# Products over the latent values in two wider bursts, with paired query products

## The chip, the cores and the metric

The kernel runs on one core of one Trainium2 chip. The metric is the device time of one execution in microseconds (us): 1379.67 before the change, the median of three runs (1377.71 to 1380.4). A core has a matrix engine (TensorE, PE in the profile), a vector engine (VectorE, DVE), a scalar engine (ScalarE, ACT), a general engine (GpSimd, POOL) and a queue that issues transfers (SyncE, SP). Each takes its own instructions strictly in their order and waits on semaphores for the others.

## The reference

Two transformer layers over 1024 tokens of width 256, in float32. Each is an attention and a block of experts, both behind a modulated layer norm and added back with a gate. What the change touches is the first attention of the first layer, which works on low-rank latents:

```
q_mid = rmsnorm(h @ q_a_w.T)                     # 192 wide
q = (q_mid @ q_b_w.T) per head: q_nope (128), q_pe (64)
kv = rmsnorm(h @ kv_a_w[:64].T)                  # 64 latents a token
k_pe = h @ kv_a_w[64:].T per head (64)
k_nope, v = kv @ kv_b_w.T per head (128, 128)
q_pe, k_pe = apply_rope(q_pe), apply_rope(k_pe)
probs = softmax((q_nope.k_nope + q_pe.k_pe) * scale)     # 16 heads
main = concat(probs @ v) @ o_w.T
```

Beside it stands a small second attention ("pattern") whose output is mixed in with a gate for each token.

## The kernel before

**Absorbed weights.** The up-projections are folded into the queries and into the output. A head's query is 128 numbers for each token: 64 that meet the 64 latents, and 64 rotated ones that meet the rotated keys. A score is one product over 128 rows. The values are the 64 latents themselves, and what the probabilities make of them is multiplied by a folded output weight, wvo. q_mid lies in q0T (its first 128 rows) and in rows 0 to 63 of mixT; rows 64 to 127 of mixT hold the latents.

**Units.** The stage runs over 16 units: 8 pairs of heads, and for each pair two halves of 512 queries (i = 0, 1). A unit has eight steps: four tiles of 128 queries for each of the two heads. A step n does these things:

- `scores(n + 2)`: two products of 128 x 128 by 512 keys into a score tile (`score_products`, line L686), the negated maximum on DVE (L690), and the exponential on ACT, which also sums (L869).
- `transposed(n)`: DVE transposes blocks of 32 x 32 of the probabilities (L877), so that keys come to stand on partitions, four groups of 32.
- Work kept in a table by step (`at(...)`): for the unit before, `over_latents` in four parts at steps 1 to 4 of the next unit; `by_latent` (four transposes on PE at L891 and ACT's copy bc at L895), which brings the inverse sums (L883, L885) into the layout of the products; and `out_part`, the four output products (L926) with an accumulation on DVE (L927).
- For the next pair of heads: `query_part` twice a unit, once for the rotated part and once for the latent part, and, where i = 0, `key_part` for both halves of the keys. `turned` rotates: ACT scales the product into t (L629) and copies four strips of 32 partitions into sw (L633), each into its partner's place; POOL multiplies and adds (L636, L637, L640). The latent part is copied straight by ACT (L675, L676).

**The products over the latents.** The array is used as eight small ones: four row groups of 32 keys and two column groups of 64. In `over_latents` row group r takes its 32 keys of block b, loads the 64 latents of those keys as weights, and streams 128 columns (four query tiles of 32 queries) of one head; column group j is head j. The four row groups add up in four PSUM tiles, and at the end DVE multiplies each of these by its piece of bc into cx (L919). One part is 8 blocks x 4 row groups x 2 heads = 64 products, in the profile 128 records, since each float32 product is two records.

**Buffers.** PSUM has two score tiles (sc) of two banks, and four tiles of one bank under the names nn and mm, handed out in turn. A unit's four row-group tiles take all four of these from the first part to the last.

**What sets the order.** In this stage only PE's order is written out by hand, by the step table. The orders of ACT, DVE and POOL are laid by a planner at build time; on the chip each engine then keeps to that order.

Of the kernel before, what the change touches and what calls it, by code (L numbers as in the profile page):

```python
# [8 lines left out]
F32 = mybir.dt.float32  # L9
# [5 lines left out]
P = 128  # L15
T = 1024
# [26 lines left out]
def adaln_two_layers(ctx: ExitStack, tc: tile.TileContext, a: dict, out: bass.AP):  # L43
    nc = tc.nc
# [7 lines left out]
    sc_tile = lambda: psum.tile([P, T], F32, tag="sc", name="sc")  # L52
    singles = ["nn", "mm"]

    def mm_tile(tag=None):
        if tag is None:
            tag = singles[0]
            singles.reverse()
        return psum.tile([P, 512], F32, tag=tag, name=tag)

    turn = [0]
# [433 lines left out]
    with pool("l0a") as l0, pool("mla") as ml:  # L495
        lnw = l0.tile([P, 2], F32, name="lnw")
        gate_b = l0.tile([P, 2], F32, name="gate_b")
        q0T = l0.tile([P, T], F32, name="q0T")
        mixT = l0.tile([P, T], F32, name="mixT")
# [5 lines left out]
        scale = (DN + DR) ** -0.5  # L505

        wq0 = l0.tile([P, NH, KVR], F32, name="wq0")
        wq1 = l0.tile([P, NH, KVR], F32, name="wq1")
# [3 lines left out]
        kv32 = ml.tile([P, 4 * NT, KVR], F32, name="kv32")  # L512
# [102 lines left out]

        kf = [[x[j].rearrange("p t d -> p (t d)") for j in range(2)], None]
        mp, wts, scs = [None], {}, {}
        qfs = {(0, 0): [l0.tile([P, 512], F32, tag=f"qf{j}", name="qf") for j in range(2)]}

        def turned(dst, at, ps, i, mul, early):  # L620
# [29 lines left out]
        def key_part(p, i, early=False):  # L650
            cols = slice(i * 512, (i + 1) * 512)
            ps = mm_tile()
            for k in range(2):
                nc.tensor.matmul(ps, wts[p][0][:, k, :], hT[i][:, k, :], start=(k == 0), stop=(k == 1))
            yield from turned(kf[p % 2], cols, ps, i, 1.0, early)

        def query_part(p, i, turn, early=False):


            cols = slice(i * 512, (i + 1) * 512)  # L660
            ps = mm_tile()
            if turn:
                if (p, i) != (0, 0):
                    qfs[p, i] = [mp[0].tile([P, 512], F32, tag=f"qf{j}", name="qf", bufs=3) for j in range(2)]
                w0, w1 = wts[p][1][:, 0, :], wts[p][1][:, 1, :]
            else:
                w0 = wq0[:, 2 * p : 2 * p + 2, :].rearrange("p h m -> p (h m)")
                w1 = wq1[:, 2 * p : 2 * p + 2, :].rearrange("p h m -> p (h m)")
            nc.tensor.matmul(ps, w0, q0T[:, cols], start=True, stop=False)
            nc.tensor.matmul(ps, w1, mixT[:, cols], start=False, stop=True)  # L670
            if turn:
                yield from turned(qfs[p, i], slice(0, 512), ps, i, scale, early)
            else:
                copy = nc.vector.tensor_copy if early else nc.scalar.copy
                copy(qfs[p, i][1][0:64, :], ps[0:64, :])  # L675
                copy(qfs[p, i][0][64:128, :], ps[64:128, :])  # L676
                yield

        def score_products(n):

# [13 lines left out]
        with pool("pat") as pat:  # L694
# [11 lines left out]
            with pool("absorb") as ab:  # L706
# [8 lines left out]
                with pool("first") as fp:  # L715
# [26 lines left out]
                    qT, kT, v = small_tensors(pat)  # L742
                    late = []
                    firsts, step, n_steps, last_divided = small_attention(pat, qT, kT, v, False, late)
                    nc.gpsimd.memset(wq1[64:128], 0.0)


                    nc.scalar.activation(own4[0:1, 0:1], one, AF.Silu)
# [1 line left out]
                    ps = mm_tile()  # L750
# [97 lines left out]
        with pool("mla1") as m1, pool("mla2", 2) as m2:  # L848
# [3 lines left out]
            def latents_of_odd():  # L852
                nc.gpsimd.tensor_copy(kf[1][0][64:128, :], mixT[64:128, :])
                nc.scalar.copy(kf[1][1][0:64, :], mixT[64:128, :])

            prs, sums, pts, cxs, bcs, rws, avs = {}, {}, {}, {}, {}, {}, {}


            units = [(p, i) for p in range(NH // 2) for i in range(2)]
# [12 lines left out]
            def transposed(n):  # L872

                u, t, j = n // 8, n % 8 // 2, n % 2
                if n % 8 == 0:
                    pts[u] = [m2.tile([P, T // 32, P], F32, tag=f"pt{k}", name="pt") for k in range(2)]
                nc.vector.transpose(  # L877
                    pts[u][j][:, :, 32 * t : 32 * t + 32], prs.pop(n).rearrange("p (b k) -> p b k", k=32)
                )

            def one_over_sums(u):
# [15 lines left out]
            def over_latents(u, part):  # L897


                n = T // 32 // 4  # L900
                if part == 0:
                    avs[u] = [mm_tile() for _ in range(4)]
                pt, av = pts[u], avs[u]
                for b in range(n * part, n * part + n):
                    for r in range(4):
                        row = slice(32 * r, 32 * r + 32)
                        for j in range(2):
                            nc.tensor.matmul(  # L908
                                av[r][64 * j : 64 * j + 64, :P], kv32[row, b, :], pt[j][row, b, :],
                                start=(b == 0), stop=(b == 4 * n - 1),  # L910
                            )
                if part < 3:
                    return
                del pts[u], avs[u]
                cxs[u] = m2.tile([P, 4, P], F32, name="cx")
                bc = bcs.pop(u)
                for r in range(4):
                    q = slice(32 * r, 32 * r + 32)
                    nc.vector.tensor_mul(  # L919
                        cxs[u][:, :, q], av[r][:, :P].rearrange("p (t q) -> p t q", t=4), bc[:, :, q]  # L920
                    )

            def out_part(u, t):
                p, i = units[u]
# [10 lines left out]
            def at(n, fn, *args):  # L935
                beside.setdefault(n, []).append((fn, args))


            def over_tiles(n, parts):

                for k in range(3):
                    at(n + k, lambda: next(parts, None))

            for u, (p, i) in enumerate(units):
                n = 8 * u
                if u + 1 < len(units):
                    at(n + 8, by_latent, u)
                for part in range(4):
                    at(n + 9 + part, over_latents, u, part)
                    if u + 1 == len(units) and part == 1:  # L950

                        at(n + 9 + part, by_latent, u, lambda: sc_tile()[:, :512])
                for t, m in enumerate((14, 15, 16, 16)):
                    at(n + m, out_part, u, t)
                if p + 1 < NH // 2:
                    if i == 0:
                        at(n, weights_of, p + 1)
                    over_tiles(n + 5, query_part(p + 1, i, True))
                    over_tiles(n + 6, query_part(p + 1, i, False))
                    if i == 0:  # L960
                        over_tiles(n + 6, key_part(p + 1, 0))
                        over_tiles(n + 7, key_part(p + 1, 1))
            def reload():
                for i in range(2):
                    nc.sync.dma_start(x[i], xv[:, 4 * i : 4 * i + 4, :])

            over_tiles(1, query_part(0, 1, True))
            over_tiles(3, query_part(0, 1, False))
            at(4, latents_of_odd)
            at(112, reload)  # L970
            last = 8 * len(units)
            at(last, residual, 0, gates_bc[0][:, :HID])
# [320 lines left out]
    with tc.manual_schedule(engines={mybir.EngineType.PE}):  # L1293
        wts = [golden(0), None]
# [16 lines left out]
        parts = projections(0, [0], False)  # L1311
# [177 lines left out]
```

## Time and profile before

| what | before |
|---|---|
| median of three runs | 1379.67 us |
| profiled execution | 1377.59 us |
| its span, first to last instruction | 1375.8 us |
| granted TensorE clock | 0.992 |
| first score to last product over latents | 316.8 to 818 us |
| 13 units between 371.2 and 774.5 us | 403.3 us |
| two successive units in the steady state | 62.03 us |

In the lines from the profile, L908 is line 908 of the kernel above. A group's line gives the engine, what it writes and reads, shapes, how many there were, busy time and mean duration in ns, then the engine's idle time before these instructions and what ended it. In a timeline the first column is the start in us from the span's start and the second the length of the merged run of instructions; a wait stands in brackets with its releaser. Matrix products overlap in their pipeline, so what one costs PE is the distance to the next start, not the listed duration.

### The profile page before, as it was taken

To read this page: it belongs to the slowest core of one execution; us is meant where nothing else is said; L and a number is where in the kernel's file an instruction comes from. 1 tells how busy PE (TensorE), PEld (TensorE's weight loads), DVE (VectorE), ACT (ScalarE), POOL (GpSimd) and SP (SyncE) were. 2 spreads that over 40 slices of the span, in tenths; PEclk is the share of its full clock that TensorE was granted. 3 is DMA by queue.
4 is the path that set the end of the run, shared out by engine and by line. 5 is a ranking of instruction groups with operands and counts; after the bars stand their busy time and mean duration, and the time that the engine had idled before them with its cause. 6 is when DMAs were issued, how large, how long until landed. Compare 5 with 4: busy or idle time off the path is not lost. (4 is left out here: it accounts for less than half of the span.)

```text
span 1375.8 us, 33066 instructions
## 1 busy us (share of the span) xinstructions
PE 1316.5 (96%) x14664; PEld 723.0 (53%) x14664; DVE 821.1 (60%) x1259; ACT 603.7 (44%) x1083; POOL 206.6 (15%) x194
## 2 busy tenths in 40 slices
PE   8999999998999999999999989999999998999998
PEld 6543324324555555555555565565556454466665
DVE  3668887836676676767676764444466666143222
ACT  4436665655655646454655323111034644511111
POOL 2000000041424324141424011000000031010000
PEclk9999999999999999999999999999999999999999
DMA  9210000000000000000001202222120000224441
GB/s 261 76 33 1 1 1 1 1 1 16 10 2 10 6 7 6 6 6 6 2 3 41 71 16 70 81 75 77 59 59 22 2 1 1 92 91 149 151 155 54
DMA packets 56601, 59.34 MB, mean 43 GB/s; under 512 B 15047, under 2 KB 42184, under 8 KB 56458
## 3 DMA queue, kind: packets, MB, share of 16 engines
q1 hardware_dynamic: 55914, 57.22, 13.7%
q8 instruction: 115, 1.88, 0.5%
q14 instruction: 28, 0.23, 0.1%
q10 hardware_dynamic: 544, 0.00, 0.0%
HBM read 55.05 MB, written 1.12 MB: 41 GB/s over the span
## 5 line engine op out<-in xcount | busy, mean ns | idle before, releaser
L323 DVE TENSOR_REDUCE mx<-sc 128x2 f32<-128x1024 f32 (+3 forms) x224 | 239.9, 1106 | 52.0 <-PE sc L317 18.1
L869 ACT ACTIVATE pr<-sc,nmax 128x1024 f32<-128x1024 f32 x128 | 142.5, 1113 | 216.3 <-DVE nmax L690 210.1
L877 DVE STREAM_TRANSPOSE pt<-pr 128x1024 f32<-128x1024 f32 x128 | 158.9, 1242 | 122.1 <-ACT pr L869 122.1
L317 PE MATMUL sc<-kT,qT 32*128 32x512 f32 (+3 forms) x896 | 208.4, 594 | 21.0 <-DVE mx L323 20.8
L351 PE MATMUL mm<-q,kT 32*128 32x512 f32 (+3 forms) x388 | 193.1, 603 | 3.3 <-DVE t L627 1.7
L351 PE MATMUL nn<-q,kT 32*128 32x512 f32 (+3 forms) x388 | 192.5, 606 | 0.7 <-DVE qf L676 0.5
L690 DVE TENSOR_REDUCE nmax<-sc 128x1 f32<-128x1024 f32 x128 | 153.8, 1203 | 14.2 <-PE sc L686 10.8
L908 PE MATMUL mm<-pt,kv 32*64 32x128 f32 x4096 | 135.2, 274 | 5.2 <-ACT bc L895 5.2
L361 ACT ACTIVATE pt<-mm 128x512 f32<-128x512 f32 (+2 forms) x194 | 108.3, 558 | 71.4 <-PE nn L351 47.8
L908 PE MATMUL nn<-pt,kv 32*64 32x128 f32 x4096 | 135.4, 274 | 4.3 <-issue 3.0
L908 PEld LDWEIGHTS mm<-pt,kv 32*64 32x64 f32 x4096 | 117.2, 130 | 30.1 <-issue 23.1
L908 PEld LDWEIGHTS nn<-pt,kv 32*64 32x64 f32 x4096 | 116.9, 130 | 28.2 <-issue 21.8
L361 ACT ACTIVATE pt<-nn 128x512 f32<-128x512 f32 (+2 forms) x194 | 108.3, 558 | 53.1 <-PE mm L351 21.0
L686 PE MATMUL sc<-kf,qf 128*128 128x512 f32 x256 | 124.0, 607 | 1.1 <-ACT pr L869 1.1
L686 PE MATMUL sc<-x,qf 128*128 128x512 f32 x256 | 123.3, 606 | 1.4 <-ACT pr L869 1.4
L317 PEld LDWEIGHTS sc<-kT,qT 32*128 32x128 f32 x896 | 68.2, 186 | 103.4 <-DVE mx L323 87.3
L636 POOL TENSOR_TENSOR t<-t,cos 128x512 f32<-128x512 f32 x32 | 41.2, 1289 | 523.5 <-ACT sw L633 267.8
L1243 DVE TENSOR_TENSOR he<-he,row 128x512 f32<-128x512 f32 x46 | 31.7, 692 | 132.9 <-ACT he L1235 99.9
L1235 ACT ACTIVATE he<-sc,b 128x512 f32<-128x512 f32 x43 | 29.5, 687 | 123.7 <-PE sc L1234 123.7
L1234 PE MATMUL sc<-hT,w 128*128 128x512 f32 x172 | 80.7, 593 | 0.0
L633 ACT COPY sw<-t 32x512 f32<-32x512 f32 x116 | 71.4, 616 | 2.0
L686 PEld LDWEIGHTS sc<-x,qf 128*128 128x128 f32 x256 | 45.5, 189 | 50.5 <-issue 46.4
(361 smaller groups left out, 2014.9 us busy)
## 6 DMA issues: line engine op xcount, KB each, us to landing
w<-in_moe_w_dram SPq DMA_DIRECT2D x50, 256.0 KB
w<-in_wg_dram SPq DMA_DIRECT2D x16, 256.0 KB
w<-in_wu_dram SPq DMA_DIRECT2D x16, 256.0 KB
w<-in_wd_dram SPq DMA_DIRECT2D x16, 256.0 KB
row<-gD SPq DMA_DIRECT2D x14, 256.0 KB
wm<-in_wmod_dram SPq DMA_DIRECT2D x6, 512.0 KB
x<-in_x_dram SPq DMA_DIRECT2D x4, 512.0 KB
wo<-in_o_dram SPq DMA_DIRECT2D x1, 2048.0 KB
```

The lines of the kernel that those rows point to most:

```text
L317: nc.tensor.matmul(sc[:, i, :n], qT[r, g, qt * P : (qt + 1) * P], kT[r, g, c * 512 : c * 512 + n], start=True, stop=not diag,)
L323: nc.vector.tensor_reduce(mx[:, qi, c, 2 * pair : 2 * pair + 2], sc[:, :, :n], AX.X, ALU.max)
L351: nc.tensor.matmul(ps[:, q0:], kT[r, g, kc * P : (kc + 1) * P], state[u]["q2"][r, q0:], start=True, stop=not diag,)
L361: nc.scalar.activation(pt[:, 2 * pair + i, q0:], ps[:, q0:], AF.Exp)
L633: copy(sw[32 * (s ^ 1) : 32 * (s ^ 1) + 32, :], t1[32 * s : 32 * s + 32, :])
L636: nc.gpsimd.tensor_mul(t1, t1, cos[:, cols])
L686: nc.tensor.matmul(sc[:, c], qfs[p, i][j][:, t * P : (t + 1) * P], kf[p % 2][j][:, c], start=True, stop=True)
L690: nc.vector.tensor_reduce(nmax, sc, AX.X, ALU.max, negate=True)
L869: nc.scalar.activation(pr, sc, AF.Exp, bias=nmax, accum_out=sums[u][:, t, j : j + 1])
L877: nc.vector.transpose(pts[u][j][:, :, 32 * t : 32 * t + 32], prs.pop(n).rearrange("p (b k) -> p b k", k=32))
L908: nc.tensor.matmul(av[r][64 * j : 64 * j + 64, :P], kv32[row, b, :], pt[j][row, b, :], start=(b == 0), stop=(b == 4 * n - 1),)
L1234: nc.tensor.matmul(ps, w1[:, k, :], hT[i][:, k, :], start=(k == 0), stop=(k == 1))
```

## The change

The products over the latents:

- The two column groups no longer stand for the two heads. Column group c takes every other block of 32 keys, and each product streams both heads' columns, 256 instead of 128. A unit has half as many products, each twice as wide, in two parts (steps 1 and 3) instead of four.
- Head j's sum is therefore split over both column groups. The transposed probabilities lie in one tile with four slots, so placed that column group 0 streams head 0 then head 1, and column group 1 head 1 then head 0. At the end ACT copies the first 128 columns of each row group's tile, two DVE adds bring in the crossed halves, and one multiplication of the whole by bc runs on POOL (for the last unit on DVE).

The queries:

- `query_parts` makes both query products of a unit at one step and in two tiles: the two with 128 rows first, then the two last chunks of 64 rows, one on rows 64 to 127 (latent part) and one on rows 0 to 63 (rotated part). For this, rows 0 to 63 of wq1 and of mixT are copied into their rows 64 to 127 once (`last_of_q_mid_twice`); a clearing of wq1's lower rows on POOL goes.
- Query pieces before that copy run their last chunk on rows 0 to 63 alone.

The table: the later pieces of the keys' rotation are put at steps further on, and `by_latent` of the last unit goes ahead of its second part.

```diff
+        def query_products(ps, p, i, turn, k):
+            lower = both[0] and not turn and k
+            row = (slice(0, P), slice(64, P) if lower else slice(0, 64))[k]
+            if turn:
+                w = wts[p][1][row, k, :]
+            else:
+                w = (wq0, wq1)[k][row, 2 * p : 2 * p + 2, :].rearrange("p h m -> p (h m)")
+            q = (q0T, mixT)[k][row, i * 512 : (i + 1) * 512]
+            nc.tensor.matmul(ps, w, q, start=(k == 0), stop=(k == 1))
...
+        def query_parts(p, i):
+            qfs[p, i] = [mp[0].tile([P, 512], F32, tag=f"qf{j}", name="qf", bufs=3) for j in range(2)]
+            pts = [mm_tile() for _ in range(2)]
+            for k in range(2):
+                for turn in range(2):
+                    query_products(pts[turn], p, i, turn, k)
+            parts = turned(qfs[p, i], slice(0, 512), pts[1], i, scale, False)
+            next(parts)
+            latent_dims(p, i, pts[0])
+            yield
+            yield from parts
...
-                    nc.gpsimd.memset(wq1[64:128], 0.0)
...
+            def last_of_q_mid_twice():
+                both[0] = True
+                nc.vector.tensor_copy(wq1[64:128], wq1[0:64])
+                nc.vector.tensor_copy(mixT[64:128, :], mixT[0:64, :])
...
-                    pts[u] = [m2.tile([P, T // 32, P], F32, tag=f"pt{k}", name="pt") for k in range(2)]
+                    pts[u] = m2.tile([P, T // 64, 4, P], F32, name="pt")
+
                 nc.vector.transpose(
-                    pts[u][j][:, :, 32 * t : 32 * t + 32], prs.pop(n).rearrange("p (b k) -> p b k", k=32)
+                    pts[u][:, :, slice(1, 3) if j else slice(0, 4, 3), 32 * t : 32 * t + 32],
+                    prs.pop(n).rearrange("p (b c k) -> p b c k", c=2, k=32),
                 )
...
-                n = T // 32 // 4
+                n = T // 32 // 2
...
-                for b in range(n * part, n * part + n):
+                for b in range(n * part, n * part + n, 2):
                     for r in range(4):
                         row = slice(32 * r, 32 * r + 32)
-                        for j in range(2):
+                        for c in range(2):
                             nc.tensor.matmul(
-                                av[r][64 * j : 64 * j + 64, :P], kv32[row, b, :], pt[j][row, b, :],
-                                start=(b == 0), stop=(b == 4 * n - 1),
+                                av[r][64 * c : 64 * c + 64, : 2 * P], kv32[row, b + c, :],
+                                pt[row, b // 2, 2 * c : 2 * c + 2, :].rearrange("p j q -> p (j q)"),
+                                start=(b == 0), stop=(b + 2 == 2 * n),
                             )
...
-                    nc.vector.tensor_mul(
-                        cxs[u][:, :, q], av[r][:, :P].rearrange("p (t q) -> p t q", t=4), bc[:, :, q]
-                    )
+                    by = [av[r][:, k * P : (k + 1) * P].rearrange("p (t q) -> p t q", t=4) for k in range(2)]
+                    nc.scalar.copy(cxs[u][:, :, q], by[0])
+                    for j in range(2):
+                        row, other = (slice(64 * k, 64 * k + 64) for k in (j, 1 - j))
+                        nc.vector.tensor_add(cxs[u][row, :, q], cxs[u][row, :, q], by[1][other])
+                eng = nc.vector if u + 1 == len(units) else nc.gpsimd
+                eng.tensor_mul(cxs[u], cxs[u], bcs.pop(u))
...
-                for part in range(4):
-                    at(n + 9 + part, over_latents, u, part)
+                for part in range(2):
...
+                    at(n + 9 + 2 * part, over_latents, u, part)
...
-                    over_tiles(n + 5, query_part(p + 1, i, True))
-                    over_tiles(n + 6, query_part(p + 1, i, False))
+                    over_tiles((n + 5, n + 6, n + 7), query_parts(p + 1, i))
                     if i == 0:
-                        over_tiles(n + 6, key_part(p + 1, 0))
-                        over_tiles(n + 7, key_part(p + 1, 1))
+                        over_tiles((n + 6, n + 8, n + 9), key_part(p + 1, 0))
+                        over_tiles((n + 7, n + 10, n + 11), key_part(p + 1, 1))
...
+            at(4, last_of_q_mid_twice)
```

## The prediction

> **What bounds the kernel now.** I read the page first (who is busy, costliest groups), then the busy time by stretch, then the timeline of TensorE (PE) and of ScalarE (ACT) over one unit.
>
> ```profile
> PE 1316.5 (96%) x14664; PEld 723.0 (53%) x14664; DVE 821.1 (60%) x1259; ACT 603.7 (44%) x1083; POOL 206.6 (15%) x194
> ...
> L908 PE MATMUL mm<-pt,kv 32*64 32x128 f32 x4096 | 135.2, 274 | 5.2 <-ACT bc L895 5.2
> ```
> ```profile
> 371.20:774.50 403.30, 394.41 (x7384) 224.70 (x7381) 285.03 (x338) 219.79 (x373) 126.30 (x100) 1.00 0.05 15
> ```
>
> The second fence is busy time from 371.2 us (end of unit 0's last burst) to 774.5 (unit 13's): length, then PE, weight loads, DVE, ACT, POOL. PE works through 394.4 of 403.3 us and the granted clock is 1.00: PE sets the pace of these thirteen units. What one item costs it is the distance between starts, not the duration of a row:
>
> ```profile
> 599.76 1.88 PE L686 MATMUL sc<-x,qf 128*128 128x512 f32 x4
> 601.48 0.59 PE L926 MATMUL mm<-wvo,cx 128*128 128x256 f32 x2
> 601.91 0.59 PE L926 MATMUL nn<-wvo,cx 128*128 128x256 f32 x2
> 602.35 0.60 PE L891 MATMUL mm<-ident,rw 128*128 128x128 f32 x4
> 602.78 1.88 PE L686 MATMUL sc<-x,qf 128*128 128x512 f32 x4
> 604.59 0.32 PE L908 MATMUL nn<-pt,kv 32*64 32x128 f32 x2
> ...
> 605.93 0.33 PE L908 MATMUL mm<-pt,kv 32*64 32x128 f32 x2 [0.88 <-ACT bc L895]
> ...
> 607.84 1.98 PE L686 MATMUL sc<-x,qf 128*128 128x512 f32 x4
> 609.75 0.32 PE L908 MATMUL nn<-pt,kv 32*64 32x128 f32 x2
> ...
> 611.78 1.98 PE L686 MATMUL sc<-x,qf 128*128 128x512 f32 x4
> ```
>
> A score is 601.48 - 599.76 = 1.72 us, an output product 0.43, the four transposes 0.43. With a burst behind it a score takes 609.75 - 607.84 = 1.91, and a burst 611.78 - 609.75 = 2.03. A burst is 64 products over 8 array tiles, each two records of 128 columns: 16 rounds of 0.109 (the spacing of the 128-column L891) = 1.74. So each visit to the small tiles costs 0.28 + 0.19 = 0.47 beyond its arithmetic. The burst at 604.59 takes 3.25: it waits until 605.93 for ACT's copy bc. ACT's timeline says why:
>
> ```profile
> 596.80 0.60 ACT L629 ACTIVATE t<-nn 128x512 f32<-128x512 f32 x1
> 597.43 2.50 ACT L633 COPY sw<-t 32x512 f32<-32x512 f32 x4
> 599.95 1.12 ACT L869 ACTIVATE pr<-sc,nmax 128x1024 f32<-128x1024 f32 x1
> 600.96 0.19 ACT L869 ACTIVATION_READ_ACCUMULATOR pr<-sc,nmax 128x1 f32 x1
> 601.05 0.59 ACT L629 ACTIVATE t<-nn 128x512 f32<-128x512 f32 x1
> 601.67 2.50 ACT L633 COPY sw<-t 32x512 f32<-32x512 f32 x4
> 604.20 1.11 ACT L869 ACTIVATE pr<-sc,nmax 128x1024 f32<-128x1024 f32 x1
> 605.21 0.19 ACT L869 ACTIVATION_READ_ACCUMULATOR pr<-sc,nmax 128x1 f32 x1
> 605.30 0.58 ACT L895 COPY bc<-mm 128x512 f32<-128x512 f32 x1
> ```
>
> For some 10 us ACT works without a gap: a scaled copy and four exchange copies (3.14 in all), an exponential (1.11), and again, with bc last. Units with i = 0 make keys too ("key units", 33.27 us from burst end to burst end, this stall in them); the others ("plain", 28.76) have no such wait. 7 x 28.76 + 6 x 33.27 = 400.9; the rest of the 403.3 is a 1.86 us hole in the burst at 763.7, no engine named, and 0.4 in the first.
>
> **The change part by part.** *Two bursts instead of four.* The same columns stream: 16 rounds x 0.216 (the record spacing of the 256-column L926) = 3.46 per burst, + 0.28 = 3.74, + 0.19 on the score before. Two cost 7.86 where four cost 8.88: -1.0 per unit. The Trainium skill (TensorEngine Tiling, Instruction Overhead) states about 60 cycles beyond the columns for each matmul; by that estimate 256 records fewer, spread over 8 tiles, would give 0.8 more per unit (13 us in all). The rows contradict it: 128 columns 0.109, 256 columns 0.216. I take nothing for the smaller count.
>
> *Queries.* Four products of 0.86 (3.44) become two of 0.86 and a pair on 64 rows each, side by side. No row shows a 64-row pair; the nearest are the 32-row L317 and L351, whose four products start within 0.02 us of each other and repeat after 0.53. So 0.86 for the pair and two switches of 0.2: 2.98, -0.46. Bounds: 3.84 if the pair runs one after the other, 2.58 with free switches.
>
> *Evacuation.* Four DVE multiplies (0.2 apart) become four ACT copies (128 columns, about 0.25 each, between the 0.27 of L361's shortest and its spacing), eight DVE adds at 0.2 and one POOL multiply (1.28, L636). From the burst's end that is 2.2 on DVE, then POOL until 3.6. The skill's rule that speaks against the change (TensorEngine Tiling, PSUM Bottleneck) is that tiling leaves evacuation as the limit. Queued behind the new waits are, on ACT, the exponential of the first score (wanted at 3.5, copies done at 1.3), on DVE that score's maximum (1.9, delayed to 2.2) and on POOL the query multiplies (10.7). The first query product needs the first buffer at 3.4 and the first output product needs cx at 8.1: both are covered, by two scores and by the query block. Without that cover, taken as the limit, with PE waiting out the 2.2, it would be +1.4 per unit. I take 0.
>
> *Transposes* keep 32-element runs, with another stride between them: 1.24 kept. DVE per unit, from start to next start: eight maxima at 1.11 and transposes at 1.17, adds 1.6, four accumulations (L927) at 0.38, the sums' inverse and its spread 0.65: 22.0 of about 30.
>
> *Exchanges.* They are spread in the program, but the built order of ACT keeps all four copies directly behind their scaled copy, and in both kinds of unit both latent copies (0.58 + 0.60) now stand ahead of them: query work is one lump of 0.58 + 0.60 + 3.14 = 4.32 ahead of the next exponential. Time zero is a unit's last burst end. A score's maximum starts 0.2 after it, its exponential 1.32 after that (620.30 to 625.94 in DVE's timeline holds such a row of steps), and each score takes one of two buffers, free again when the exponential ends.
>
> Plain unit. PE: two scores 3.44, queries to 6.42, score C to 8.14, output, score D, output: 10.72. ACT: lump 6.43 to 10.75; behind it in the queue stands C's exponential, which could have begun at 9.7, and runs to 11.87. The fifth score needs C's buffer: it starts at 11.95, a stall of 1.23 (late next is D's exponential, 12.98, and nothing waits for it). Then 1.72 + 0.86 + 0.44 + 1.91 + 3.74 + 1.72 + 1.91 + 3.74 = 16.04: 28.0 instead of 28.76.
>
> Key unit. After the queries at 6.42 PE has three scores (5.16), two key products (3.44), four output products (1.72), the transposes (0.44) and the score before the burst (1.91): 19.09. ACT: 10.75 + 1.11 + 3.14 + 1.11 + 3.14 + 1.11 + bc 0.58 = 20.94. The burst loses 1.8, since three of its four row groups have buffers and do 0.1 of it before. Late next are DVE's transposes of those scores; they end at 32.2, just ahead of the next evacuation. Then 3.74 + 1.72 + 1.91 + 3.74: 32.0 instead of 33.27.
>
> Sum: 7 x 28.0 + 6 x 32.0 = 388.0, + 0.9 (half of the 1.86 hole; half as many instructions to fetch may be its cure, but nothing shows it) = 388.9 against 403.3: -14.4. Unit 14 has no queries and hangs on the score buffers: its third score waits for the first's exponential (4.7) and its fifth for the third's (9.9), with 16.0 behind that: 25.9 instead of 26.57, -0.65. Start (316.8 to 371.2): two visits fewer, one pair, -1.4; the two earlier query pieces run their last chunk on 64 rows alone, two switches of 0.2 each, of which half on the path, +0.4; the copy of 64 x 1024 into mixT (0.69, L790) lies on DVE where PE waits little: 0 to +0.7, taken as 0. The same copy of wq sits in DVE's queue at 65.7 ahead of two maxima: +0.4, of 0 to 0.7; the POOL memset removed (0.95, at 4.9) is waited for by nobody. Tail: two visits fewer -1.0, but copies, adds and a DVE multiply follow one another before the last output products, +1.0: 0, of -1 to +2. Behind it the engines' order is unchanged. Total: -1.4 + 0.4 + 0.4 - 14.4 - 0.65 = -15.7, say -16. The profiled execution is 1377.59 (span 1375.8 and 1.8 around it), 2.1 below the median; the difference goes on the median: 1379.67 - 16 = 1363.5.
>
> **Rivals.** A, the exchanges don't stall PE: 26.77 and 30.2 per unit, another 7 x 1.23 + 6 x 1.8 = 19.4: 1344. For it: PE is the only engine above 75% in the stretch. Against it: ACT's order, and a bc wait of 0.88 already there with the same work. B, the 64-row pair runs in sequence: +0.86 in 14 units, 12 us: 1375.5. For it: the form isn't in the trace; against it the 32-row rows. C, slower: the strided write makes the transpose dearer. Each 0.1 us is 0.8 per unit; DVE's 22.0 fills the 30 at +1.0, and from about +1.1 (2.3 instead of 1.24) a unit passes the 31.0 of before. At double cost DVE has 31.4, with some waits left about 33: 14 x 2 = +28, 1408. Against it: same run length, same count of elements.
>
> **How the numbers follow.** Forecast 0.67, A 0.12, B 0.13, C 0.08. The forecast's own range is 1356 to 1370 (0.5 us per unit either way); A's 1338 to 1350, B's 1371 to 1380. The range 1347 to 1377 leaves out C and the outer parts of A and B. A difference under 0.2% (2.8 us) can't be told from none: faster 0.89, same 0.03, slower 0.08.
>
> **What would show it.** Distances: score to score 1.91 and a burst 3.74; query block 2.98; a stall of about 1.2 ended by an exponential (pr) before a plain unit's fifth score; bc ending a wait of nearly 2 us in each key unit's first burst; transposes at 1.24. The prediction is wrong if ACT's lump doesn't reach PE, if the pair's products start 0.4 apart, or if DVE shows no gaps.

## The result and the profile after

The changed kernel takes 1364.82 us in the median (four runs, 1364.39 to 1368.62), against 1379.62 for the kernel before beside it: ratio 0.9901, with a 95% interval of 0.9881 to 0.9921. Taken again later it was 0.9890 (0.9873 to 0.9906). The change makes the kernel 1.0% faster; the forecast was 1363.5, with 1347 to 1377 as its range.

The profiled execution took 1364.39 us, span 1362.6. The first lines of the page after (busy time of each engine; costliest groups of the products over the latents):

```profile
PE 1297.5 (95%) x10568; PEld 694.6 (51%) x10568; DVE 848.4 (62%) x1326; ACT 616.7 (45%) x1147; POOL 224.3 (16%) x208
...
L936 PE MATMUL mm<-pt,kv 32*64 32x256 f32 x2048 | 124.5, 381 | 5.6 <-ACT bc L923 5.5
```

The busy time by stretch, for the thirteen units between the last bursts of units 0 and 13, for unit 14, and from there to the first product of the experts (start and end, length, then PE, weight loads, DVE, ACT, POOL, with the granted clock as the third number from the end):

```profile
370.35:757.96 387.61, 374.06 (x4061) 199.73 (x4053) 304.82 (x391) 229.94 (x424) 142.33 (x113) 1.00 0.05 14
757.96:784.06 26.10, 24.07 (x309) 13.31 (x301) 23.09 (x31) 10.83 (x21) 1.26 (x1) 1.00 0.01 2
784.06:812.12 28.06, 22.90 (x316) 15.59 (x309) 21.17 (x49) 5.92 (x15) 3.94 (x8) 0.88 0.04 9
```

Thirteen units take 387.6 us where they took 403.3, and PE's share of them is 374.1 of 387.6, where it was 394.4 of 403.3: PE has less to do, and waits a little more. Of these three lines only the last has a clock below 1.00. Start distances of PE in the steady state give 27.96 us for a plain unit (forecast 28.0, before 28.76) and 31.98 for a key unit (forecast 32.0, before 33.27).

PE in a plain unit of the changed kernel:

```profile
373.89 1.02 PE L668 MATMUL nn<-q0T,wq 128*128 128x512 f32 x2
374.75 1.02 PE L668 MATMUL mm<-q0T,wpe 128*128 128x512 f32 x2
375.70 0.69 PE L668 MATMUL nn<-mixT,wq 64*128 64x512 f32 x1
375.70 0.69 PE L668 MATMUL mm<-mixT,wpe 64*128 64x512 f32 x1
...
376.76 1.98 PE L708 MATMUL sc<-kf,qf 128*128 128x512 f32 x4
378.58 0.59 PE L958 MATMUL nn<-wvo,cx 128*128 128x256 f32 x2
379.01 1.88 PE L708 MATMUL sc<-kf,qf 128*128 128x512 f32 x4
...
382.47 0.70 PE L708 MATMUL sc<-kf,qf 128*128 128x512 f32 x1 [1.15 <-ACT pr L895]
```

The two 64-row products start together (375.70), and the query block takes 376.76 - 373.89 = 2.87, with 0.10 more on the score behind it: 2.97, forecast 2.98. The fifth score then waits 1.15 for an exponential; from start to start the output product ahead of it takes 382.47 - 380.73 = 1.74 instead of 0.43, so the stall costs 1.31 (forecast 1.23). ACT in the same unit shows the lump, the six copies of the query work that stand together:

```profile
376.86 0.58 ACT L672 COPY qf<-nn 64x512 f32<-64x512 f32 x1
377.45 0.58 ACT L673 COPY qf<-nn 64x512 f32<-64x512 f32 x1
378.06 0.60 ACT L630 ACTIVATE t<-mm 128x512 f32<-128x512 f32 x1
378.68 2.50 ACT L634 COPY sw<-t 32x512 f32<-32x512 f32 x4
381.21 1.12 ACT L895 ACTIVATE pr<-sc,nmax 128x1024 f32<-128x1024 f32 x1
```

The exponential that the score waits for runs from 381.21 to 382.32, that is 10.86 to 11.97 after the last burst's end at 370.35; the forecast had 10.75 to 11.87. In a key unit the same work makes bc late in the first burst:

```profile
417.86 0.65 PE L936 MATMUL nn<-pt,kv 32*64 32x256 f32 x4
419.42 0.43 PE L936 MATMUL mm<-pt,kv 32*64 32x256 f32 x2 [0.91 <-ACT bc L923]
```

That burst takes 5.64 instead of 3.64, so the wait costs 2.0 (forecast 1.8); the 0.91 is only what is left after three of the four row groups have done what they could.

### The profile page after: what moved, and what is told of

Read it like the earlier page. It is cut to its first block, busy times and chain, and to the rows that moved or that the text cites. A ratio compares the mean times of both kernels' runs of the same rounds, so it can differ in the third digit from the quotient of the medians.

```text
span 1362.6 us, 25036 instructions
## 1 busy us (share of the span) xinstructions
PE 1297.5 (95%) x10568; PEld 694.6 (51%) x10568; DVE 848.4 (62%) x1326; ACT 616.7 (45%) x1147; POOL 224.3 (16%) x208
## 4 chain that ended last, share of the span: by engine, by line
PE 73%; ACT 12%; DVE 10%; issue 2%; SPq 1%; DMA 1%; POOL 0%; DVEq 0%; ACTq 0%
PE sc L317 10%; PE sc L708 8%; PE mm L936 6%; PE sc L1267 5%; PE mm L383 5%; ACT pr L895 5%; DVE mx L323 4%; ACT sw L634 4%; PE sc L1151 4%; PE nn L1283 3%; PE nn L936 3%; PE mm L1283 3%; PE nn L383 2%; DVE cx L951 2%; PE mm L1151 2%
## 5 line engine op out<-in xcount | busy, mean ns | idle before, releaser
L904 DVE STREAM_TRANSPOSE pt<-pr 128x1024 f32<-128x1024 f32 x128 | 157.0, 1236 | 51.5 <-ACT pr L895 51.5
L936 PE MATMUL mm<-pt,kv 32*64 32x256 f32 x2048 | 124.5, 381 | 5.6 <-ACT bc L923 5.5
L708 PE MATMUL sc<-kf,qf 128*128 128x512 f32 x256 | 120.7, 604 | 6.6 <-ACT pr L895 6.6
L936 PE MATMUL nn<-pt,kv 32*64 32x256 f32 x2048 | 124.9, 382 | 1.9 <-DVE pt L904 1.9
L936 PEld LDWEIGHTS mm<-pt,kv 32*64 32x64 f32 x2048 | 85.2, 133 | 29.3 <-issue 11.7
L936 PEld LDWEIGHTS nn<-pt,kv 32*64 32x64 f32 x2048 | 84.9, 133 | 20.1 <-issue 12.3
L708 PEld LDWEIGHTS sc<-kf,qf 128*128 128x128 f32 x256 | 45.6, 189 | 62.3 <-issue 55.2
```

Source lines behind the costliest of these rows:

```text
L708: nc.tensor.matmul(sc[:, c], qfs[p, i][j][:, t * P : (t + 1) * P], kf[p % 2][j][:, c], start=True, stop=True)
L904: nc.vector.transpose(pts[u][:, :, slice(1, 3) if j else slice(0, 4, 3), 32 * t : 32 * t + 32], prs.pop(n).rearrange("p (b c k) -> p b c k ...
L936: nc.tensor.matmul(av[r][64 * c : 64 * c + 64, : 2 * P], kv32[row, b + c, :], pt[row, b // 2, 2 * c : 2 * c + 2, :].rearrange("p j q -> p ...
```

## The experiments

The table gives, for each kernel whose units differ, the steady distances from a unit's last burst to the next one's, and the time; the runs that only change the stage's end follow in their section. The sections below say what each was.

| kernel | plain unit | key unit | both | median us | ratio to before (95%) |
|---|---|---|---|---|---|
| before | 28.76 | 33.27 | 62.03 | 1379.62 | |
| changed | 27.96 | 31.98 | 59.94 | 1364.82 | 0.9901 (0.9881 to 0.9921) |
| wide bursts alone | 27.42 | 31.87 | 59.29 | 1358.91 | 0.9853 (0.9830 to 0.9876) |
| query part alone | 29.57 | 33.49 | 63.06 | 1387.71 | 1.0063 (1.0048 to 1.0078) |
| changed, ACT's order by hand | 28.86 | 30.02 | 58.88 | 1364.39 | 0.9896 (0.9881 to 0.9910) |
| the same, key steps moved | 27.76 | 30.02 | 57.78 | 1352.50 | 0.9804 (0.9785 to 0.9823) |
| the same, ten products at the end | 27.76 | 30.02 | 57.78 | 1350.49 | 0.9786 (0.9768 to 0.9804) |
| the same, 64-row products not paired | 28.59 | 31.26 | 59.85 | 1364.88 | 0.9890 (0.9871 to 0.9909) |
| query part alone, ACT's order by hand, key steps moved | 28.88 | 31.59 | 60.47 | 1372.17 | 0.9944 (0.9931 to 0.9957) |
| wide bursts, four visits a unit | 30.25 | 34.8, 38.06 | | 1416.43 | 1.0256 (1.0226 to 1.0286) |

### Which part of the change pays

The wide bursts alone: the changed kernel with the queries, the keys' steps and the clearing of wq1 put back.

```diff
-                    over_tiles((n + 5, n + 6, n + 7), query_parts(p + 1, i))
+                    over_tiles(n + 5, query_part(p + 1, i, True))
+                    over_tiles(n + 6, query_part(p + 1, i, False))
...
-            at(4, last_of_q_mid_twice)
```

> The change without its query part: wide products in two bursts and the new evacuation, but the queries, the keys' rotation and the clearing of wq1 as before the change. By the prediction's sum the bursts are worth -1.0 per unit and the hole -1.9, so about -17 over the stage, less the 5 that the tail gave back in the changed kernel: 1379.6 - 12 = 1367 to 1368. Plain unit 27.8 (28.76 before), key unit 32.3 (33.27 before), bursts 3.64 with 1.91 on the score before them. If instead the wide products themselves are worth nothing and the gain came from the queries: 1379, plus the tail's 5, 1384. If the evacuation through ACT, DVE and POOL costs PE something that the query part only covered: above 1372.

Measured: 1358.91, units of 27.42 and 31.87, some 9 us below what I expected and 5.9 us *faster than the whole change*. The two units gain 2.74, 1.37 for each, where I had 1.0. What PE waited for in the units, first in the changed kernel and then in this one (what waits and for whom, us in total, times, longest):

```profile
PE sc L708 <- ACT pr L895: 8.1, 7, 1.2
PE mm L936 <- ACT bc L923: 5.5, 6, 0.9
```

```profile
PE mm L910 <- ACT bc L897: 2.6, 6, 0.4
```

Without the query part no score waits for an exponential, and bc is late by 0.4 instead of 0.9. The evacuation through ACT, DVE and POOL is in both.

The query part alone, on the kernel before:

```diff
-                    over_tiles(n + 5, query_part(p + 1, i, True))
-                    over_tiles(n + 6, query_part(p + 1, i, False))
+                    over_tiles((n + 5, n + 6, n + 7), query_parts(p + 1, i))
...
+            at(4, last_of_q_mid_twice)
```

> The query part of the change alone: paired 64-row products, the copies into rows 64 to 127 and the new steps of the keys' rotation, on the kernel before with its four bursts. If the pair's gain of 0.5 per unit reaches the end: 14 x 0.5 = 7, 1372 to 1373. If ACT's lump (both latent copies and four exchange copies ahead of the next exponential) stalls PE here as in the changed kernel, 1.1 in a plain unit's fifth score and more at a key unit's bc, the gain is eaten: 1378 to 1386, with a wait ended by pr in the fifth score of a plain unit. I hold the second for likelier.

Measured: 1387.71, slower than before by 0.63% (0.48 to 0.78). Its waits:

```profile
PE sc L708 <- ACT pr L895: 8.1, 7, 1.2
PE mm L934 <- ACT bc L921: 6.7, 6, 1.1
PE mm L934 <- issue: 2.2, 1, 2.2
```

The same wait of 1.15 in each plain unit as in the changed kernel (8.1 in 7). The pair saves 0.46 and the lump that comes with it costs 1.31 from start to start: a plain unit gets longer by 0.81. (The line with "issue" is a wait inside a burst for which the profile names no releaser, like the hole of 1.86 before the change.) So the change is one part that gains about 1.4 per unit and one that gives 0.1 to 0.5 of it back (0.2 to 0.8 on the kernel before).

### Is it ACT's order?

The changed kernel with ACT's order in this stage laid by hand, as the program has it. Nothing else moves.

```diff
-            with tc.manual_schedule(engines={mybir.EngineType.PE}):
+            with tc.manual_schedule(engines={mybir.EngineType.PE, mybir.EngineType.Activation}):
```

> The changed kernel with ACT's order in this stage written out as the program has it, so that the exchange copies really stand two and two behind later exponentials. If the lump of six copies is what stalls PE (the forecast's mechanism; its absence was rival A): the waits of 1.15 in the fifth score and of 0.9 to 2 at bc go, plain unit 26.8 to 27.0, key unit 30.2 to 30.6, and 19 in all: 1345 to 1348. If PE's stalls have another cause, or another copy takes the lump's place: 1360 to 1366.

Measured: 1364.39, as good as no change, and yet the two waits that I had named are gone. Key units fall to 30.02, what rival A gave them (30.2). Plain units rise to 28.86, and the waits say for whom:

```profile
PE sc L708 <- POOL kf L641: 5.0, 4, 1.3
PE sc L708 <- POOL x L641: 3.8, 3, 1.3
```

In program order the last two exchange copies of the second key half stand at step 11, behind the four copies of cx. In one such unit they are done at 494.6, but on POOL the multiplies for that half now stand behind the one for cx, which waits for DVE until 496.1: they start at 497.3, and the score that needs these keys waits 1.26. At the stage's start PE waits 1.92 once for the copy into mixT, which now waits for the latents' copy at step 4. At its end unit 14 takes 2.4 more, with PE at half rate for 3.4 us of it. So the lump was what stalled PE, as the first theory had it, and new waits took its place, which the second had left room for. To tell this from a plain lack of time on ACT or POOL, the second key half's exchanges go to steps 9 and 10, ahead of cx's copies, and the latents' copies to step 1:

```diff
-                        over_tiles((n + 7, n + 10, n + 11), key_part(p + 1, 1))
+                        over_tiles((n + 7, n + 9, n + 10), key_part(p + 1, 1))
...
-            at(4, latents_of_odd)
+            at(1, latents_of_odd)
```

> The changed kernel with ACT's order written out as in the run before, and two steps of the table moved: the second key piece's exchanges at steps 9 and 10 (not 10 and 11), and the copies of the latents for odd pairs at step 1 (not 4). In the run with ACT's order alone the two waits that I forecast for the lump were gone, and two others stood in their place: 1.25 us in each pair of units for the second key half on POOL (its multiplies stood behind cx's), and 1.92 once for mixT. If that is all that ate the gain, two units take 57.2 to 57.4 us (59.94 in the changed kernel) and the whole 1346 to 1349. If ACT's or POOL's work is simply too much for any order: two units near 59, 1360 to 1365.

Measured: 1352.50, 12.3 below the changed kernel; two units take 57.78 (59.94 before these edits). POOL no longer ends a wait in the units, and of 13.6 us of waits for pr and bc these are left:

```profile
PE sc L708 <- ACT pr L895: 3.4, 7, 0.7
```

The order was the cause: the same instructions, moved within ACT's queue (POOL's order in this trace is that of the changed kernel), take 12 us less. The forecast for this run was 1346 to 1349, and the part that missed is in the plain unit, 27.76, where 57.2 to 57.4 for two units left at most 27.4. DVE's timeline there, from the last burst's end at 488.27:

```profile
488.02 1.25 DVE L904 STREAM_TRANSPOSE pt<-pr 128x1024 f32<-128x1024 f32 x1 [0.91 <-ACT pr L895]
489.28 0.59 DVE L951 TENSOR_TENSOR cx<-cx,nn 64x128 f32<-64x128 f32 x2
...
491.73 2.36 DVE L712 TENSOR_REDUCE nmax<-sc 128x1 f32<-128x1024 f32 x2
494.29 2.38 DVE L904 STREAM_TRANSPOSE pt<-pr 128x1024 f32<-128x1024 f32 x2 [0.20 <-ACT pr L895]
...
497.12 1.22 DVE L712 TENSOR_REDUCE nmax<-sc 128x1 f32<-128x1024 f32 x1
```

DVE works for 10 us almost without a gap: a transpose, the eight adds, two maxima, two transposes, the inverse sums, and only then the third score's maximum, though that score ends at 496.5. Its exponential then starts at 498.43, 10.2 after the burst's end; in the changed kernel it was 10.9. With ACT's lump out of the way DVE's queue is the next to be late. Whether it is the adds that make it late was not tried.

The same two edits, on the query part alone:

> The query part alone on the kernel before (1387.7), with ACT's order written out and the moved key steps. If the lump in ACT's order is what turned the query part into a loss: plain unit near 28.3, key unit near 32 (29.57 and 33.49 in the run of the query part alone, 28.76 and 33.27 before): 1366 to 1372. If the loss comes from something else, such as query products that wait for the evacuation of the burst one score ahead of them: 1380 to 1388.

Measured: 1372.17, against 1387.71 with the planner's order. Beside its own runs of the kernel before, the query part is a loss of 8.6 us with the planner's order, and the query part together with ACT's order and two moved steps is a gain of 8.2. Units of 28.88 and 31.59: the key unit did as forecast, the plain one stayed 0.6 above and is no shorter than before the change (28.76). The gain is not the query part's own: the key unit is 1.68 shorter, and 1.22 of that is the wait for bc that the kernel before had too (its first burst took 3.25, a free one 2.03). ACT's order by hand on the kernel before, and on the wide bursts alone, was not run. So these runs show that the lump turned the query part into a loss, and leave open whether the query part pays once the order is mended.

### What the pair of 64-row products is worth

The kernel of 1350.49 (ACT's order, moved steps, and ten products at the end of which more below), with the four query products in plain order:

```diff
-            for k in range(2):
-                for turn in range(2):
+            for turn in range(2):
+                for k in range(2):
                     query_products(pts[turn], p, i, turn, k)
```

> The combined kernel (1350.5) with its four query products of a unit in the plain order, rotated part after latent part, so that the two 64-row products no longer stand next to each other and can't run side by side; all else the same. If the pairing is worth what the query block shows (2.86 + 0.10 on the score behind it, against 4 x 0.86 = 3.44 with its switches), two units take 1.0 to 1.6 us more than the 57.78 of the combined kernel: 1357 to 1362. If ACT's and DVE's work has become the limit there, PE only waits less: two units within 0.3, 1350 to 1352.

Measured: 1364.88, 14.4 more, and 2.07 for two units: the first theory, and more than it forecast. PE in a plain unit:

```profile
496.89 1.02 PE L668 MATMUL nn<-q0T,wq 128*128 128x512 f32 x2
497.84 1.12 PE L668 MATMUL nn<-mixT,wq 64*128 64x512 f32 x2
498.89 1.12 PE L668 MATMUL mm<-q0T,wpe 128*128 128x512 f32 x2
499.95 1.12 PE L668 MATMUL mm<-mixT,wpe 64*128 64x512 f32 x2
501.00 0.70 PE L708 MATMUL sc<-kf,qf 128*128 128x512 f32 x1
```

The block takes 501.00 - 496.89 = 4.11, and 0.10 more on the score behind it, where four products of 0.86 are 3.44. The 0.77 between them is four changes between 128 and 64 rows at 0.19, half of it ahead of the change and half behind; the paired block has two of them (0.86 + 0.86 + 0.86 + 0.38 = 2.96). So the pair is worth 1.24 against the same products apart, and 0.48 against products filled up to 128 rows, as the kernel before has them. Both units lose by it, the key unit all of it (1.24) and the plain one 0.83, so PE is still the limit of the key unit after the order was mended, and for the most part of the plain one. A kernel with the mended order and products filled up was not run; the 0.48 is a sum.

### What a visit to the small tiles costs

The kernel with the wide bursts alone, its products in four bursts of 32 at steps 1 to 4 instead of two of 64:

```diff
-                n = T // 32 // 2
+                n = T // 32 // 4
...
-                if part == 0:
+                if part < 3:
                     return
...
-                    at(n + 9 + 2 * part, over_latents, u, part)
+                    at(n + 9 + part, over_latents, u, part)
```

> The kernel with the wide products alone (queries as before the change, 1358.9), but its 256-column products in four bursts of 32 instead of two of 64. If the gain is the visit's fixed cost (the forecast: 0.28 + 0.19 for each visit), two visits more cost 0.9 to 1.2 per unit, 14 to 18 in all: 1373 to 1377. If the gain is the smaller count of instructions or the smoother stream of wide products: 1359 to 1362.

Measured: 1416.43, far outside both. The price of a visit can be read from PE's distances all the same. A burst of 8 rounds takes 1.91 and one of 16 takes 3.64: a round is (3.64 - 1.91) / 8 = 0.216, as I had it, and what lies outside the rounds is 1.91 - 1.73 = 0.18, with 0.19 on the score before. That is 0.37 for a visit with wide products; with narrow ones it was 0.47. Four visits cost 8.4 a unit, two cost 7.66: the visits explain 0.74 of the 2.83 that a plain unit lost. The next part of it is this (PE first, then DVE):

```profile
467.16 1.98 PE L686 MATMUL sc<-x,qf 128*128 128x512 f32 x4
469.86 1.10 PE L669 MATMUL mm<-q0T,wpe 128*128 128x512 f32 x2 [0.71 <-issue]
```

```profile
469.17 0.58 DVE L925 TENSOR_TENSOR cx<-cx,mm 64x128 f32<-64x128 f32 x2
469.79 0.58 DVE L925 TENSOR_TENSOR cx<-cx,nn 64x128 f32<-64x128 f32 x2
```

The last burst now ends one score ahead of the query products, not two. The first of them needs a tile that DVE's adds still read, and starts at 469.86, when the first two adds (469.17 to 469.75) are done. Here the profile names no releaser; in six other units it names these adds (what waits and for whom, 402 to 805 us):

```profile
PE nn L669 <- DVE cx L925: 4.6, 6, 0.8
PE mm L669 <- issue: 4.3, 6, 0.7
```

The two scores are the cover that the prediction named; with one of them the evacuation costs PE 0.7 to 0.8 a unit. Among the rest are waits for exponentials and for bc and, from unit 6 on, key units at 38.06 with the clock at 0.91. This run therefore doesn't separate the visits from the width by its total, and only its rows do.

### The stage's end

From unit 14's last burst to the first product of the experts the changed kernel takes 28.06 us; before it was 22.79. PE in that stretch of the changed kernel, at unit 15's first burst:

```profile
792.29 0.65 PE L936 MATMUL nn<-pt,kv 32*64 32x256 f32 x4 [1.95 <-DVE pt L904]
...
793.85 0.69 PE L936 MATMUL mm<-pt,kv 32*64 32x256 f32 x2
...
794.33 0.64 PE L936 MATMUL mm<-pt,kv 32*64 32x256 f32 x2
```

Two things are in it. Until 793.85 the fourth row group has no tile, since its tile is read by DVE's last accumulation for unit 14 until 793.8. And from there the rounds follow each other at 0.40 to 0.48, not 0.216. The busy time by stretch gives the clock for this burst and for the output products behind the last one:

```profile
793.10:797.20 4.10, 4.02 (x70) 2.43 (x76) 4.00 (x8) 0.00 (x0) 0.00 (x0) 0.58 0.00 0
...
806.90:812.00 5.10, 5.05 (x23) 4.50 (x24) 3.19 (x6) 0.00 (x0) 1.53 (x6) 0.67 0.14 36
```

PE runs at about half rate in both, each time behind a wait of 2 to 2.5 us. To test whether standing idle does it, added products of 128 x 128 by 256 columns keep PE at work, with nothing reading them:

```diff
+            def kept_busy(n):
+                ps = sc_tile()
+                for _ in range(n):
+                    nc.tensor.matmul(ps[:, :HID], ident, wvo[:, 0, :], start=True, stop=True)
...
+                if u + 2 == len(units):
+                    at(n + 14, kept_busy, 2)
+                    at(n + 16, kept_busy, 5)
+                if u + 1 == len(units):
+                    at(n + 14, kept_busy, 6)
```

> The changed kernel with thirteen products of 128 x 128 by 256 columns added in the three waits at the stage's end (2 ahead of unit 14's output products, 5 ahead of unit 15's first burst, 6 ahead of its output products); their results are not used. If PE's half rate there (0.58 of the clock granted from 793.1 to 797.2, 0.67 from 806.9 to 812) is the answer to PE having stood idle, the burst goes from 6.8 to about 3.7 and the products after the second burst from 0.85 to 0.43 each: -4 to -5.5, 1359 to 1361. If the half rate has another cause, or the added products only lengthen the chain: 1364 to 1368.

Measured: 1364.01 (0.9889, 0.9875 to 0.9904), the time of the second theory. Yet in the trace the clock is 1.00 in the whole stretch, but the first two products wait 1.74 for a score buffer and push unit 14's output products back by 2.2 against the changed kernel's trace; the stretch is 26.0 instead of 28.06. Without those two, and with four ahead of the burst:

> The changed kernel with ten added products at the stage's end whose results are not used: 4 (1.7 us) in the wait of 1.95 ahead of unit 15's first burst, 6 (2.6 us) in the wait of 2.54 ahead of its output products; none ahead of unit 14's output products, where the first trial made PE wait for a score buffer and cost 2.2. If standing idle is what halves PE's rate: the burst 3.7 to 4.3 instead of 6.8, the output products 0.43 apart instead of 0.85, -4 to -4.8 in all: 1360 to 1361. If the rate falls all the same: 1364 to 1366.

Measured: 1364.58 (0.9877, 0.9857 to 0.9898), not the 1360 to 1361 of the first theory, with 1358.9 in the profiled execution and 1362.64 to 1365.48 in the others. Side by side with the changed kernel once more:

> The changed kernel once more, beside the next run on the same chip: 1364.8 as before, its tail (end of unit 14's last burst to the first expert product) 28.1 us in the profiled execution.

> The changed kernel with the ten added products at the stage's end once more, side by side with the changed kernel. Its first profiled execution was 5.5 below that of the changed kernel with a tail of 24.75 instead of 28.06, but its other four executions were not. If the saved half rate reaches the end in every execution: 3.3 below the run beside it. If it does only in some, or is given back elsewhere: 0 to 1.5 below.

Measured: 1364.05 for the changed kernel (0.9890, 0.9873 to 0.9906) and 1362.97 with the added products (0.9884, 0.9870 to 0.9899). Both stretches, first of the changed kernel, then with the added products:

```profile
785.42:814.51 29.09, 23.93 (x317) 17.11 (x309) 21.16 (x49) 5.92 (x15) 5.10 (x13) 0.85 0.08 15
```

```profile
784.34:809.09 24.75, 23.86 (x337) 17.40 (x329) 20.77 (x49) 5.91 (x15) 3.57 (x8) 1.00 0.02 6
```

```profile
794.12 0.43 PE L936 MATMUL mm<-pt,kv 32*64 32x256 f32 x2
...
794.39 0.38 PE L936 MATMUL mm<-pt,kv 32*64 32x256 f32 x2
```

With PE kept at work the clock stays at 1.00, the rounds follow at 0.27 (last fence) and then at 0.22, and the stretch is 24.75 in both traces of this kernel, 3.3 below the 28.06. That PE's idleness there brings the half rate is shown. In the medians 0.2 and 1.1 of it are seen, and the intervals overlap: how much of the 3.3 reaches the end in most executions stays open. It need not be the same in each: from this stretch on, the first trace of the changed kernel has two spells of half rate of 3.4 us, and the second one of 3.4 and one of 10.2.

The ten products on top of ACT's order and the moved steps:

> ACT's order with the moved key steps, and the ten added products at the stage's end. If the lump and the half rate are two separate causes their gains add: 1342 to 1345. If one hides behind the other or if both theories fail: 1350 to 1365.

Measured: 1350.49 (0.9786, 0.9768 to 0.9804), 2.0 below the run without them, and above the 1342 to 1345 that I expected, mostly because the mended order gave 12 us and not 19. In the profiled executions the stretch at the end is 1.7 shorter (24.75 against 26.42); the intervals of the two kernels overlap, so that the gains add is likely and not shown. It has the lowest median here, 1.0% below the changed kernel.

## Why the prediction was right, point by point

- **The time** (1363.5 against 1364.82) is right, and most of its terms are. The differences, from the two profiled executions: 0.9 later at the first score (forecast 0.4; it lies between 316.8 and 320.4 in the traces of all these kernels), -15.7 in the thirteen units (forecast -14.4), -0.5 in unit 14 (-0.65), -1.7 at the start (-1.0) and +5.3 at the end (0), -1.5 behind (0): -13.2 in the span. That the sum came so close is in part luck: the units gave 1.3 more than forecast, and the 1.5 behind the stage, where the program is the same, goes with the clock (the trace before has PE at half rate for 6.8 us there, the trace after for 3.4); both made up for part of what the end lost.
- **Two bursts**: right in kind, mis-sized. A visit costs 0.37 with wide products, 0.47 with narrow ones, so a burst is 3.64 and not 3.74, and two of them with their scores save 1.22 and not 1.0; alone the part gains 1.37 a unit. Within the rounds nothing is gained from the smaller count of instructions: the round of 256 columns is 0.216, twice the 0.109 of 128.
- **Queries**: 2.97 against 2.98. The products start together, so rival B is out.
- **Transposes** stay at 1.24 (mean 1236 ns): rival C is out.
- **The lump** is 4.32 on ACT (376.86 to 381.18), as summed; PE's stalls are 1.31 in the plain unit against 1.23, 2.0 in the key unit against 1.8. Rival A's 30.2 is what the key unit reaches once ACT's order is mended (30.02), so the lump was its whole loss; of the plain unit's 1.2 only 0.2 came back.
- **The evacuation** was costed at nothing, under two scores. That holds in the changed kernel, though DVE's adds are 0.3 apart and not 0.2 and DVE is done with them 2.8 after the burst's end, not 2.2. With one score of cover it cost 0.7 to 0.8, where the prediction had 1.4 for no cover at all; once ACT's lump is gone DVE is late behind it. The Trainium skill's section (TensorEngine Tiling, PSUM Bottleneck) says no more than that the copies out of PSUM may become the bottleneck, and with two scores of cover they were not.
- **The hole** of 1.86 is gone altogether, where I took half. Such waits with no releaser stand in bursts of all three kernels with narrow products (1.6 before the change, 2.2 and 0.9 in the two runs of the query part) and in no burst with wide ones, be it two bursts or four. So they go with the narrow products and not with the number of visits; what causes them no run here shows.
- **The tail is the term that failed**: "copies, adds and a DVE multiply follow one another before the last output products, +1.0: 0, of -1 to +2". It measured +5.3. Of this 1.72 is no loss: the last burst of a unit now comes a step sooner, so one score more is counted behind unit 14 and one fewer ahead of unit 0's end (60 records of score products come before that end in the trace before and 56 after, four to a score; so the start's -1.7 is that score, and its forecast gain of about 1 is not seen). Of the other 3.5, 3.3 is PE at half rate, by what the filled waits gave back. The chain itself cost about what was said; that waits of 2 us in it would halve PE's rate was not in the sum.
- **What the prediction didn't ask** is what each part was worth with the wait that it brings. Its own numbers held it: -0.46 for the pair and +1.23 for the lump in a plain unit make the query part a loss there. The sum was right, and the finding that half of the change works against the other half went unsaid.

## What to carry to other kernels

Add up each part of a change together with the waits that it brings, not by kinds of cost over the whole: a part that shortens the busy engine can still lose. Spreading work over the steps of a program can come to nothing if a planner lays the order of the engine that does it; look at that engine's order as built, and when it is laid by hand, look for the next queue (here POOL's, behind cx) that the moved work now stands in. Behind a wait of some 2 us (1.95 and 2.54 here) look at the rate of the matrix engine and not only at the length of the wait.

## What the runs showed of the hardware

- PE's rate can halve behind waits of 1.95 and 2.54 us: the clock was 0.58 and 0.67 over the stretches behind them, and 1.00 where the same waits were filled. The length of the wait alone doesn't decide it: in the run with moved key steps the same wait of 1.95 was followed by a burst at full rate (5.15, with the wait for the fourth tile in it). The clock records of the traces show what does go with it. In each trace the half rate comes in spells of 3.41 us, or two or three times that, and up to 1340 us all of them begin and end on one grid of 3.41 us; ahead of a spell lies a window of that grid in which PE did little. Here are the window with the wait of 1.95 and the next one, in the changed kernel and in the run with moved key steps (length, PE, weight loads, DVE, ACT, POOL, with the clock as the third number from the end):

```profile
790.38:793.79 3.41, 1.48 (x12) 0.58 (x12) 3.41 (x8) 0.20 (x2) 0.00 (x0) 1.00 0.00 0
793.79:797.21 3.42, 3.36 (x64) 2.24 (x72) 3.32 (x7) 0.00 (x0) 0.00 (x0) 0.50 0.00 0
```

```profile
778.50:781.91 3.41, 1.59 (x8) 1.06 (x6) 3.21 (x4) 1.83 (x4) 0.00 (x0) 1.00 0.02 5
781.91:785.33 3.42, 3.20 (x76) 2.11 (x84) 3.35 (x8) 0.00 (x0) 0.00 (x0) 1.00 0.00 0
```

  The second grid cuts a little off the wait, and PE's share of the window is 47% instead of 43%. From 310 to 1340 us, in the fourteen traces together, 22 windows at full rate had PE busy for 46% of the time or less, and all 22 are followed by half rate; of twelve with 47 to 51% five are; of those above, only five, each with a burst on the small tiles in it. This is read from the traces; no run shifted a wait against the grid. The Trainium skill (TensorE: Matmul & The Clock Gate, What's actually happening) puts the half rate behind an idle window of about 3.4 us and says that the windows run free of the kernel. The windows are seen here, but 43% of work in one didn't keep the rate up.
- A product on 64 of 128 rows that stands alone costs more than one on all 128 rows filled up with zeros: 0.86 and two changes of 0.19, or 1.24, against 0.86 (from the unpaired run's block of 4.11 and the 0.10 behind it). With a partner on the other half of the rows, the two together cost that 1.24.
